# Graph attention on one core: a second chain of accumulating DMAs, later steps for what waits on transfers, and small matrix products in place of transposes

## The chip, the cores and the metric

One core of a Trainium2 chip. The metric is the device time of one launch in microseconds (us). A core has five engines with a queue each: TensorE (PE in the profile, its weight loads PEld), VectorE (DVE), ScalarE (ACT), GpSimd (POOL) and SyncE (SP). Transfers run on 16 DMA engines, whichever queue issued them. The rounds ran on several chips, each with the kernel before beside the others; its median moved between 2603.27 and 2607.61 us, so a difference between two rounds is good to some 4 us.

## The reference

Two graph attention layers over 2048 nodes and 8 graphs, then a normalisation. The matrix of scores is 2048 x 2048 for each of the 8 graphs and 4 heads, and once more per graph in the second layer.

```python
def _gat_layer(h, mask, b):
    scores = einsum('...nd,...md->...nm', h, h)
    scores = where(mask, scores, NEG)
    attn = softmax(scores, axis=-1)
    return einsum('...nm,...md->...nd', attn, h) + b

mask = graph + eye(N) > 0
h    = einsum('bnc,hdc->bhnd', x, Wh)
cat  = heads side by side of _gat_layer(h, ...)
h2   = einsum('bnk,dk->bnd', leaky_relu(cat, 0.2), Wo)
z2   = leaky_relu(_gat_layer(h2, ...), 0.2)
out  = layernorm(z2) * gamma + beta
return layernorm(x + out)
```

## The kernel before

Two heads (or two graphs) are worked on together, each with 64 of the 128 partitions. A *step* `(c, m)` makes the scores of 128 nodes `m` against a *chunk* of 512 nodes `c`, subtracts the mask, takes the exponential `e` (128 x 1024, 512 KB), and, three steps later (`LAG`), multiplies it with the values into two PSUM banks `O[c]`. 16 steps are a chunk, four chunks a unit, and there are 16 units of the first layer and 4 of the second.

```python
def scores(self, c, m):
    ps = spsum(...)                                   # two PSUM buffers, tag "s"
    ... 4 matmuls of 64x64 on 64x512 into ps          # PE
    nc.vector.tensor_tensor(e, ps, mask[c]..., OP.subtract)      # DVE
    nc.scalar.activation(e, e, AF.Exp, ...)                      # ACT
    return e

def values(self, c, m, e):
    if m == 0:
        self.O[c] = [opsum(...) for r in range(2)]    # banks last used by chunk c - 2
    ... 4 matmuls into self.O[c][r]
```

The softmax needs the sum of `e` over all `m`. It is brought down to a few terms first, in two ways at once: GpSimd adds tiles (2.4 us each), and an accumulating DMA adds one tile onto another in SBUF (0.9 us of GpSimd to issue). A DMA onto a chain's first tile must wait for the one before it on the same tile.

```python
CHAINS = (((0, 3, 6, 9, 12),), ((0, 4, 8, 12), (2, 6, 10, 14)))     # first, second layer
...
def add_up(self, c, m, e):
    for k, chain in enumerate(CHAINS[self.second]):
        if m == chain[0]:
            self.first[k] = e; self.terms[c].append(e); return
        if m in chain:
            nc.gpsimd.dma_start(out=self.first[k], in_=e, accum_op=OP.add); return
    ... else nc.gpsimd.tensor_tensor(self.acc, self.acc, e, OP.add)
```

The rest of a chunk is done by jobs that are placed so many steps after its start, among the steps of the next chunks. `sums` multiplies the terms with ones; four small DMAs of 2 KB (`zt`) spread the result over partitions; `invert` takes the reciprocal, which goes to DRAM (`rd`) and comes back broadcast (`z`, 128 KB); `scale` multiplies `O[c]` by it. `project`, then `keep` (first layer) or `norm` (second layer) finish, and they are the last to read `O[c]`.

```python
LATE = [(19, "join"), (20, "join2"), (21, "fifth"), (21, "sums"), (22, "leaky"), (25, "invert"),
        (29, "scale"), (31, "project"), (32, "keep")]
NORM = [32, 33, 34, 36, 42, 43, 45, 46, 47, 50]
for t in range(total + 64):
    ... scores of step t;  values and add_up of step t - LAG;  then the jobs placed at t
```

Of the kernel before, what the change touches and what calls it, by code (L numbers as in the profile page):

```python
# [354 lines left out]
def fast_kernel(ctx: ExitStack, tc: tile.TileContext, x, adj, Wh, bh, Wo, bo, gamma, beta, out, flag):  # L355
# [14 lines left out]
    CHAINS = (((0, 3, 6, 9, 12),), ((0, 4, 8, 12), (2, 6, 10, 14)))  # L370
# [18 lines left out]
    def opsum(name):  # L389
        return psum.tile([P, W], F32, tag="o", name=name, bufs=4)  # L390
# [40 lines left out]
    def load_x(bp):  # L431
        sts = []
        for h in range(2):
            st = slot([P, NB // 2, 2, C], F32, f"x{bp}_{h}")
            for b2 in range(2):
                nc.sync.dma_start(out=st[:, :, b2, :],
                                  in_=x[2 * bp + b2, h * N // 2:(h + 1) * N // 2].rearrange("(c p) d -> p c d", p=P))
            sts.append(st)
        return sts

    def transpose_x(bp, sts, h):
        if h == 0:
            xT[bp] = big.tile([P, N], F32, tag="xT", name=f"xT{bp}", bufs=1)
        p = spsum(f"px{bp}_{h}")
        for k in range(NB // 2):
            nc.tensor.transpose(p[:, k * P:(k + 1) * P], sts[h][:, k].rearrange("p b d -> p (b d)"), ident)
        nc.scalar.copy(xT[bp][:, h * 1024:(h + 1) * 1024], p)

    x0 = load_x(0)
# [40 lines left out]
    for q in range(HP):  # L490
        nc.tensor.transpose(pw[:, q * P:(q + 1) * P], wst[:, q].rearrange("p r c -> p (r c)"), ident)
        nc.tensor.transpose(pw[:, 256 + q * D:256 + (q + 1) * D], wos[:, q * P:(q + 1) * P], ident[:D, :D])
    nc.vector.tensor_copy(whT, pw[:, :H * D])
    nc.vector.tensor_copy(woT.rearrange("p q d -> p (q d)"), pw[:, 256:256 + HP * D])
# [17 lines left out]
    class Unit:  # L512
# [6 lines left out]

        def prepare(self, h):  # L520

            n = self.n
            if h == 0:
                self.hT = h2T[self.bp] if self.second else maps[self.bp, self.hp][:, self.b2, :]
                self.hN = big.tile([P, NB, P], F32, tag="hN", name=f"hN{n}")
            p = spsum(f"pn{n}_{h}")
            for k in range(NB // 2):
                m = h * NB // 2 + k
                nc.tensor.transpose(p[:, k * P:(k + 1) * P], self.hT[:, m * P:(m + 1) * P], ident)  # L529
            b = bob.rearrange("p r d -> p (r d)") if self.second else bhb[:, self.hp * P:(self.hp + 1) * P]  # L530
            nc.vector.tensor_add(self.hN[:, h * NB // 2:(h + 1) * NB // 2, :], p.rearrange("p (m d) -> p m d", d=P),  # L531
                                 b.unsqueeze(1).to_broadcast([P, NB // 2, P]))
# [13 lines left out]
        def values(self, c, m, e):  # L546
            if m == 0:
                self.O[c] = [opsum(f"o{self.n}_{c}_{r}") for r in range(2)]
            for j in range(2):
                for r in range(2):  # L550
                    rows = slice(r * 64, (r + 1) * 64)
                    nc.tensor.matmul(self.O[c][r][j * D:(j + 1) * D, :], self.hN[rows, m, j * D:(j + 1) * D],  # L552
                                     e[rows, j, :], start=(m == 0), stop=(m == NB - 1))

        def add_up(self, c, m, e):

            if m == 0:
                self.terms[c], self.first, self.acc = [], {}, None
            for k, chain in enumerate(CHAINS[self.second]):
                if m == chain[0]:  # L560
                    self.first[k] = e
                    self.terms[c].append(e)
# [8 lines left out]
            elif len(self.terms[c]) == len(CHAINS[self.second]):  # L571
                acc = accs.tile([P, 2, W], F32, tag="acc", name=f"acc{self.n}_{c}")
                nc.gpsimd.tensor_tensor(acc, self.acc, e, OP.add)  # L573
                self.acc = acc
                self.terms[c].append(acc)
            else:
                nc.gpsimd.tensor_tensor(self.acc, self.acc, e, OP.add)  # L577


        def join(self, c):  # L580

            a, b = self.O[c]
            t = wtile(f"oj{self.n}_{c}")
            nc.scalar.copy(t, a)  # L584
            self.t = t

        def join2(self, c):
            b = self.O[c][1]
            nc.vector.tensor_tensor(b, b, self.t, OP.add)  # L589

        def fifth(self, c):
            self.t = wtile(f"o5{self.n}_{c}")
            nc.scalar.mul(self.t, self.O[c][1], SLOPE)  # L593

        def leaky(self, c):
            b = self.O[c][1]
# [253 lines left out]
```

## Time and profile before

| | before |
|---|---|
| time | 2607.61 us (4 runs, 2600.8 to 2609.52) |
| PE busy / POOL busy | 96% / 85% |
| accumulating DMAs, landing after | 352, 4.9 us |
| the reciprocal's way: zt / rd / z, landing after | 1.8 / 1.4 / 3.6 us |
| first score / last value product / end | 25.7 / 2555.8 / 2604.0 us |

PE sets the pace: between the first score and the last value product it does two groups of eight matmuls per step, each 0.858 us, and any wait of PE is added to the time. Other engines matter where they make PE wait. The times from issue to landing in the DMA part of the page are medians.

### The profile page before, as it was taken

The numbers are of one execution on the slowest core, as the hardware profiler recorded it, in microseconds if no ns is written. First come the engines' busy times: TensorE is split into PE (matmuls) and PEld (weight loads), VectorE is DVE, ScalarE is ACT, GpSimd is POOL, SyncE is SP. The second block draws the span as 40 slices with busy tenths as digits, with TensorE's granted clock in tenths as the row PEclk, the third lists the DMA queues.
The fourth block names the chain that finished last, engine by engine and source line by source line (L and its number), as shares of the span: only waits on it lengthen the run. The fifth ranks groups of instructions, "written<-read, shape, count | busy, mean of one in ns | idle before, by whom it ended". The sixth has DMA issues, their size and how long they took to land.

```text
span 2604.0 us, 53831 instructions
## 1 busy us (share of the span) xinstructions
PE 2507.1 (96%) x22406; PEld 866.4 (33%) x22406; DVE 1834.2 (70%) x1813; ACT 1703.5 (65%) x1721; POOL 2214.6 (85%) x1249
## 2 busy tenths in 40 slices
PE   8999999999999999999999999999999999999993
PEld 3333333333333333333333333333333333333331
DVE  6877777677776677667767667766777777777773
ACT  6766666666666666666666666666666666666662
POOL 4779898788789998889868999888889898877996
PEclk9999999999999999999999999999999999999996
DMA  7644434334554443434455344433444443346663
GB/s 180 158 104 86 81 76 90 74 74 82 98 115 94 84 81 78 96 71 84 81 110 111 79 85 83 90 74 74 82 78 79 83 84 76 74 90 119 123 123 79
DMA packets 168991, 239.91 MB, mean 92 GB/s; under 512 B 96898, under 2 KB 113346, under 8 KB 168738
## 3 DMA queue, kind: packets, MB, share of 16 engines
q0 software_dynamic: 50864, 184.83, 37.8%
q1 hardware_dynamic: 117250, 51.36, 7.7%
q8 instruction: 177, 2.90, 0.5%
q14 instruction: 76, 0.62, 0.1%
q10 hardware_dynamic: 624, 0.20, 0.0%
HBM read 46.60 MB, written 4.52 MB: 20 GB/s over the span
## 4 chain that ended last, share of the span: by engine, by line
PE 67%; DMA 9%; POOL 5%; DVE 5%; issue 3%; ACT 3%; SPq 1%; DVEq 0%; ACTq 0%; POOLq 0%
PE s L539 32%; PE o L552 29%; DVE e L542 4%; DMA z<-rd 4%; PE pz L609 3%; POOL acc L577 3%; DMA rd<-rt 2%; DMA e<-e 2%; DMA zt<-zsb 1%; PE pn L529 1%; ACT e L543 1%; PE o L653 1%; POOL st L691 1%; SPq L618 1%; POOL y L692 1%
## 5 line engine op out<-in xcount | busy, mean ns | idle before, releaser
L543 ACT ACTIVATE e<-e,shifts 128x1024 f32<-128x1024 f32 x1280 | 1469.3, 1149 | 823.5 <-DVE e L542 801.4
L542 DVE TENSOR_TENSOR e<-s,mask 128x1024 f32<-128x1024 f32 x1280 | 1558.8, 1221 | 588.6 <-PE s L539 566.6
L577 POOL TENSOR_TENSOR acc<-acc,e 128x1024 f32<-128x1024 f32 x656 | 1605.5, 2447 | 129.8 <-ACT e L543 104.7
L552 PE MATMUL o<-e,hN 64*64 64x512 f32 x10240 | 1332.3, 591 | 0.0
L539 PE MATMUL s<-hT 64*64 64x512 f32 x8192 | 1078.5, 597 | 24.9 <-DVE e L542 22.1
L552 PEld LDWEIGHTS o<-e,hN 64*64 64x64 f32 x10240 | 392.0, 133 | 710.5 <-issue 515.4
L539 PEld LDWEIGHTS s<-hT 64*64 64x64 f32 x8192 | 289.9, 133 | 611.5 <-issue 378.5
L565 POOL DMA_DIRECT2D e<-e x352 | 320.7, 911 | 48.6 <-ACT e L543 25.4
L573 POOL TENSOR_TENSOR acc<-e,e 128x1024 f32<-128x1024 f32 x80 | 189.8, 2372 | 106.1 <-ACT e L543 99.2
L539 PE MATMUL s<-h2T 64*64 64x512 f32 x2048 | 268.8, 595 | 3.9 <-DVE e L542 3.9
L539 PEld LDWEIGHTS s<-h2T 64*64 64x64 f32 x2048 | 74.3, 133 | 147.1 <-issue 115.1
L609 PE MATMUL pz<-e,ones 128*32 128x512 f32 x448 | 100.1, 610 | 10.1 <-DMA e<-e 7.2
L636 DVE TENSOR_TENSOR z<-o,z 128x512 f32<-128x512 f32 x80 | 54.9, 687 | 72.1 <-DMA z<-rd 72.0
L609 PE MATMUL pz<-acc,ones 128*32 128x512 f32 x320 | 85.0, 610 | 9.4 <-POOL acc L577 9.4
L691 POOL TENSOR_TENSOR st<-st,mhalf 128x8 f32<-128x8 f32 x32 | 56.9, 1777 | 41.6 <-ACT st L690 41.4
L589 DVE TENSOR_TENSOR o<-o,oj 128x512 f32<-128x512 f32 x80 | 55.9, 699 | 4.5 <-ACT oj L584 2.8
L612 ACT COPY zsb<-pz 128x512 f32<-128x512 f32 x80 | 46.2, 578 | 19.0 <-PE pz L609 19.0
L597 DVE TENSOR_TENSOR o<-o,o 128x512 f32<-128x512 f32 x80 | 55.2, 690 | 0.7 <-ACT o L593 0.7
L487 DVE CAST mask<-pm 128x1024 uint8<-128x1024 bf16 x32 | 39.1, 1223 | 16.4 <-PE pm L486 15.3
L593 ACT ACTIVATE o<-o 128x512 f32<-128x512 f32 x80 | 46.3, 578 | 0.8 <-DVE o L589 0.8
L584 ACT COPY oj<-o 128x512 f32<-128x512 f32 x80 | 45.5, 569 | 0.3
L531 DVE TENSOR_TENSOR hN<-pn,bhb 128x1024 f32<-128x1024 f32 x32 | 39.1, 1223 | 8.6 <-PE pn L529 7.8
(72 smaller groups left out, 616.6 us busy)
## 6 DMA issues: line engine op xcount, KB each, us to landing
e<-e POOLq DMA_DIRECT2D x352, 512.0 KB, 4.9
z<-rd SPq DMA_DIRECT2D x160, 128.0 KB, 3.6
adj<-in_adj_dram SPq DMA_DIRECT2D x32, 512.0 KB, 7.8
zt<-zsb SPq DMA_DIRECT2D x320, 2.0 KB, 1.8
x<-in_x_dram SPq DMA_DIRECT2D x16, 256.0 KB, 6.6
xr<-in_x_dram SPq DMA_DIRECT2D x32, 128.0 KB, 5.6
out_dram<-y SPq DMA_DIRECT2D x32, 128.0 KB, 2.1
rd<-rt SPq DMA_DIRECT2D x80, 4.0 KB, 1.4
```

Of the source, the lines that this page charges most:

```text
L539: nc.tensor.matmul(ps[k * 64:(k + 1) * 64, j, :], self.hT[rows, m * P + k * 64:m * P + (k + 1) * 64], self.hT[rows, c * W:(c + 1) * W], st ...
L542: nc.vector.tensor_tensor(e, ps, mask[c][:, m, :].unsqueeze(1).to_broadcast([P, 2, W]), OP.subtract)
L543: nc.scalar.activation(e, e, AF.Exp, bias=shifts[:, 1:2] if self.second else shifts[:, 0:1], scale=1.0)
L552: nc.tensor.matmul(self.O[c][r][j * D:(j + 1) * D, :], self.hN[rows, m, j * D:(j + 1) * D], e[rows, j, :], start=(m == 0), stop=(m == NB - 1))
L565: nc.gpsimd.dma_start(out=self.first[k], in_=e, accum_op=OP.add)
L573: nc.gpsimd.tensor_tensor(acc, self.acc, e, OP.add)
L577: nc.gpsimd.tensor_tensor(self.acc, self.acc, e, OP.add)
L589: nc.vector.tensor_tensor(b, b, self.t, OP.add)
L597: nc.vector.tensor_tensor(b, b, self.t, OP.max)
L609: nc.tensor.matmul(pz[q:q + 32, :W], ones, terms[s * half + k][:, j, :], start=(k == 0), stop=(k == half - 1), tile_position=(0, q))
L636: nc.vector.tensor_tensor(dst, self.O[c][1], self.z[c], OP.mult)
L691: nc.gpsimd.tensor_tensor(st[:, 2, :], st[:, 1, :], mhalf, OP.pow)
```

## The change

It means to relieve GpSimd by more accumulating DMAs (576 instead of 352), to give the transfers more steps to land, to avoid changes of TensorE's tiling by doing transposes and the centring as 64x64 products, and to start the steps earlier by placing the first map projections among them. Cut to its core:

```diff
-    CHAINS = (((0, 3, 6, 9, 12),), ((0, 4, 8, 12), (2, 6, 10, 14)))
+    CHAINS = (((0, 3, 6, 9, 12), (1, 5, 8, 11)), ((0, 3, 6, 9, 12), (1, 4, 7, 10, 13)))
+    JOINED = (1, 2)                      # first layer: GpSimd adds the second chain to its own sum
...
-        return psum.tile([P, W], F32, tag="o", name=name, bufs=4)
+        return psum.tile([P, 2, W], F32, tag="o", name=name)
...
+    def turn(dst, src, rows):
+        nc.tensor.matmul(dst, src, ident[rows, rows], start=True, stop=True)
...  prepare: 8 transposes of 128x128 become 32 products of 64x64; centring and x likewise
-        nc.scalar.copy(xT[bp][:, h * 1024:(h + 1) * 1024], p)
+        nc.scalar.copy(xT[bp][:, h * 1024:(h + 1) * 1024].rearrange("c (r p k) -> c r k p", r=2, p=64), pv)
...
+            any_ = nc.vector if self.n == len(units) - 1 and c == NC - 1 else nc.gpsimd   # last norm on DVE
...
+    at(0, lambda: project_x(0, 0, 1))    # first projections and transposes among the steps
...
-    LATE = [(19, "join"), (20, "join2"), (21, "fifth"), (21, "sums"), (22, "leaky"), (25, "invert"), (29, "scale"), (31, "project"),
-            (32, "keep")]
-    NORM = [32, 33, 34, 36, 42, 43, 45, 46, 47, 50]
+    LATE = [(19, "join"), (20, "join2"), (21, "fifth"), (22, "leaky"), (22, "sums"), (26, "invert"), (31, "scale"),
+            (33, "project"), (34, "keep")]
+    NORM = [34, 35, 36, 37, 46, 47, 53, 54, 55, 62]
...  the check of the sums (judge) moves ahead of the last norm
```

More of the change, by code (lines that the diff above doesn't have):

```diff
@@ L429, in fast_kernel, with load_x, transpose_x @@
     xT = {}
-    def load_x(bp):
-        sts = []
-        for h in range(2):
-            st = slot([P, NB // 2, 2, C], F32, f"x{bp}_{h}")
-            for b2 in range(2):
-                nc.sync.dma_start(out=st[:, :, b2, :],
-                                  in_=x[2 * bp + b2, h * N // 2:(h + 1) * N // 2].rearrange("(c p) d -> p c d", p=P))
-            sts.append(st)
-        return sts
-    def transpose_x(bp, sts, h):
+    def turn(dst, src, rows):
+        nc.tensor.matmul(dst, src, ident[rows, rows], start=True, stop=True)
+    def load_x(bp, h):
+        st = slot([P, 2, NB // 2, C], F32, f"x{bp}_{h}")
+        for b2 in range(2):
+            nc.sync.dma_start(out=st[:, b2], in_=x[2 * bp + b2, h * N // 2:(h + 1) * N // 2].rearrange("(p k) d -> p k d", p=P))
+        return st
+    def transpose_x(bp, st, h):
         if h == 0:
@@ L444, in transpose_x @@
         p = spsum(f"px{bp}_{h}")
+        pv = p.rearrange("c (r k p) -> c r k p", r=2, p=64)
         for k in range(NB // 2):
-            nc.tensor.transpose(p[:, k * P:(k + 1) * P], sts[h][:, k].rearrange("p b d -> p (b d)"), ident)
-        nc.scalar.copy(xT[bp][:, h * 1024:(h + 1) * 1024], p)
-    x0 = load_x(0)
+            for b2 in range(2):
+                for r in range(2):
+                    rows = slice(r * 64, (r + 1) * 64)
+                    turn(pv[b2 * C:(b2 + 1) * C, r, k, :], st[rows, b2, k, :], rows)
+        nc.scalar.copy(xT[bp][:, h * 1024:(h + 1) * 1024].rearrange("c (r p k) -> c r k p", r=2, p=64), pv)
+    x0 = [load_x(0, h) for h in range(2)]
     ws = slot([P, 1024], F32, "ws")
@@ L490, in fast_kernel @@
     for q in range(HP):
-        nc.tensor.transpose(pw[:, q * P:(q + 1) * P], wst[:, q].rearrange("p r c -> p (r c)"), ident)
-        nc.tensor.transpose(pw[:, 256 + q * D:256 + (q + 1) * D], wos[:, q * P:(q + 1) * P], ident[:D, :D])
-    nc.vector.tensor_copy(whT, pw[:, :H * D])
-    nc.vector.tensor_copy(woT.rearrange("p q d -> p (q d)"), pw[:, 256:256 + HP * D])
+        nc.tensor.transpose(pw[:, 0, q * P:(q + 1) * P], wst[:, q].rearrange("p r c -> p (r c)"), ident)
+        nc.tensor.transpose(pw[:, 1, q * D:(q + 1) * D], wos[:, q * P:(q + 1) * P], ident[:D, :D])
+    nc.vector.tensor_copy(whT, pw[:, 0, :H * D])
+    nc.vector.tensor_copy(woT.rearrange("p q d -> p (q d)"), pw[:, 1, :HP * D])
     maps = {}
@@ L518, in __init__, with hT @@
             self.terms, self.zt, self.z, self.O, self.ln = {}, {}, {}, {}, {}
+        @property
+        def hT(self):
+            return h2T[self.bp] if self.second else maps[self.bp, self.hp][:, self.b2, :]
         def prepare(self, h):
@@ L523, in prepare @@
             if h == 0:
-                self.hT = h2T[self.bp] if self.second else maps[self.bp, self.hp][:, self.b2, :]
                 self.hN = big.tile([P, NB, P], F32, tag="hN", name=f"hN{n}")
             p = spsum(f"pn{n}_{h}")
+            pv = p.rearrange("p (j m d) -> p j m d", j=2, d=D)
             for k in range(NB // 2):
                 m = h * NB // 2 + k
-                nc.tensor.transpose(p[:, k * P:(k + 1) * P], self.hT[:, m * P:(m + 1) * P], ident)
-            b = bob.rearrange("p r d -> p (r d)") if self.second else bhb[:, self.hp * P:(self.hp + 1) * P]
-            nc.vector.tensor_add(self.hN[:, h * NB // 2:(h + 1) * NB // 2, :], p.rearrange("p (m d) -> p m d", d=P),
-                                 b.unsqueeze(1).to_broadcast([P, NB // 2, P]))
+                for g in range(2):
+                    for j in range(2):
+                        rows = slice(j * D, (j + 1) * D)
+                        turn(pv[g * 64:(g + 1) * 64, j, k, :], self.hT[rows, m * P + g * 64:m * P + (g + 1) * 64], rows)
+            b = bob if self.second else bhb[:, self.hp * P:(self.hp + 1) * P].rearrange("p (j d) -> p j d", d=D)
+            nc.vector.tensor_add(self.hN[:, h * NB // 2:(h + 1) * NB // 2, :].rearrange("p m (j d) -> p j m d", d=D), pv,
+                                 b.unsqueeze(2).to_broadcast([P, 2, NB // 2, D]))
         def scores(self, c, m):
@@ L547, in values @@
             if m == 0:
-                self.O[c] = [opsum(f"o{self.n}_{c}_{r}") for r in range(2)]
+                self.O[c] = opsum(f"o{self.n}_{c}")
             for j in range(2):
@@ L551, in values @@
                     rows = slice(r * 64, (r + 1) * 64)
-                    nc.tensor.matmul(self.O[c][r][j * D:(j + 1) * D, :], self.hN[rows, m, j * D:(j + 1) * D],
+                    nc.tensor.matmul(self.O[c][j * D:(j + 1) * D, r, :], self.hN[rows, m, j * D:(j + 1) * D],
                                      e[rows, j, :], start=(m == 0), stop=(m == NB - 1))
@@ L557, in add_up @@
             if m == 0:
-                self.terms[c], self.first, self.acc = [], {}, None
+                self.first, self.acc, self.made = {}, None, False
+                self.terms[c] = []
             for k, chain in enumerate(CHAINS[self.second]):
@@ L561, in add_up @@
                     self.first[k] = e
-                    self.terms[c].append(e)
                     return
@@ L570, in add_up @@
                 self.acc = e
-            elif len(self.terms[c]) == len(CHAINS[self.second]):
+            elif not self.made:
                 acc = accs.tile([P, 2, W], F32, tag="acc", name=f"acc{self.n}_{c}")
                 nc.gpsimd.tensor_tensor(acc, self.acc, e, OP.add)
-                self.acc = acc
-                self.terms[c].append(acc)
+                self.acc, self.made = acc, True
             else:
                 nc.gpsimd.tensor_tensor(self.acc, self.acc, e, OP.add)
+            if m == NB - 1:
+                k = JOINED[self.second]
+                for chain in range(k, len(self.first)):
+                    nc.gpsimd.tensor_tensor(self.acc, self.acc, self.first[chain], OP.add)
+                self.terms[c] += [self.first[j] for j in range(k)] + [self.acc]
         def join(self, c):
-            a, b = self.O[c]
-            t = wtile(f"oj{self.n}_{c}")
-            nc.scalar.copy(t, a)
-            self.t = t
+            self.t = wtile(f"oj{self.n}_{c}")
+            nc.scalar.copy(self.t, self.O[c][:, 0, :])
         def join2(self, c):
-            b = self.O[c][1]
+            b = self.O[c][:, 1, :]
             nc.vector.tensor_tensor(b, b, self.t, OP.add)
@@ L592, in fifth @@
             self.t = wtile(f"o5{self.n}_{c}")
-            nc.scalar.mul(self.t, self.O[c][1], SLOPE)
+            nc.scalar.mul(self.t, self.O[c][:, 1, :], SLOPE)
         def leaky(self, c):
-            b = self.O[c][1]
+            b = self.O[c][:, 1, :]
             nc.vector.tensor_tensor(b, b, self.t, OP.max)
@@ L635, in scale @@
             dst = self.z[c] if self.second or self.hp else z0[:, self.b2, c, :]
-            nc.vector.tensor_tensor(dst, self.O[c][1], self.z[c], OP.mult)
+            nc.vector.tensor_tensor(dst, self.O[c][:, 1, :], self.z[c], OP.mult)
         def project(self, c):
-            p = self.O[c][0]
             if self.second:
                 for i in range(CB):
-                    nc.tensor.matmul(p[:, i * P:(i + 1) * P], self.z[c][:, i * P:(i + 1) * P],
-                                     centre.rearrange("p r d -> p (r d)"), start=True, stop=True)
+                    for g in range(2):
+                        for b2 in range(2):
+                            rows = slice(b2 * D, (b2 + 1) * D)
+                            nc.tensor.matmul(self.O[c][g * 64:(g + 1) * 64, b2, i * D:(i + 1) * D],
+                                             self.z[c][rows, i * P + g * 64:i * P + (g + 1) * 64], centre[rows, b2, :],
+                                             start=True, stop=True)
                 return
+            p = self.O[c][:, 0, :]
             if self.hp == 0 or c % 2 == 0:
@@ L662, in keep @@
                 k = c - 1 + g
-                nc.scalar.copy(h2T[self.bp][rows, k * W:(k + 1) * W], self.O[c][0][g * D:(g + 1) * D, :])
+                nc.scalar.copy(h2T[self.bp][rows, k * W:(k + 1) * W], self.O[c][g * D:(g + 1) * D, 0, :])
         def norm(self, c, part):
@@ L674, in norm @@
                 self.y = ytile(f"y{n}_{c}")
-                nc.scalar.copy(self.y, self.O[c][0])
+                o = self.O[c][:, :, :W // 2]
+                nc.scalar.copy(self.y.rearrange("p (b i) -> p b i", b=2), o)
                 self.sq = wtile(f"sq{n}_{c}")
-                nc.scalar.square(self.sq, self.O[c][0])
+                nc.scalar.square(self.sq.rearrange("p (b i) -> p b i", b=2), o)
                 self.st = small.tile([P, 6, K], F32, tag="st", name=f"st{n}_{c}", bufs=2)
                 self.xr = ytile(f"xr{n}_{c}")
-                xv = self.xr.rearrange("p (i b d) -> p i b d", b=2, d=D)
+                xv = self.xr.rearrange("p (b i d) -> p b i d", b=2, d=D)
                 for b2 in range(2):
-                    nc.sync.dma_start(out=xv[:, :, b2, :],
+                    nc.sync.dma_start(out=xv[:, b2],
                                       in_=x[2 * self.bp + b2, c * W:(c + 1) * W, :].rearrange("(i p) d -> p i d", p=P))
@@ L691, in norm @@
                 nc.gpsimd.tensor_tensor(st[:, 2, :], st[:, 1, :], mhalf, OP.pow)
-                nc.gpsimd.tensor_tensor(v(y), v(y), col(st[:, 2, :]), OP.mult)
+                any_.tensor_tensor(v(y), v(y), col(st[:, 2, :]), OP.mult)
             elif part == 3:
-                nc.gpsimd.tensor_tensor(v(y), v(y), row(gam), OP.mult)
-                nc.gpsimd.tensor_tensor(v(y), v(y), row(bet), OP.add)
-                nc.gpsimd.tensor_tensor(y, y, xr, OP.add)
+                any_.tensor_tensor(v(y), v(y), row(gam), OP.mult)
+                any_.tensor_tensor(v(y), v(y), row(bet), OP.add)
+                any_.tensor_tensor(y, y, xr, OP.add)
             elif part == 4:
@@ L700, in norm @@
                 nc.scalar.mul(st[:, 4, :], st[:, 3, :], -1.0 / D)
-                nc.gpsimd.tensor_tensor(v(y), v(y), col(st[:, 4, :]), OP.add)
+                any_.tensor_tensor(v(y), v(y), col(st[:, 4, :]), OP.add)
             elif part == 6:
@@ L705, in norm @@
             elif part == 9:
-                yv = y.rearrange("p (i b d) -> p i b d", b=2, d=D)
+                yv = y.rearrange("p (b i d) -> p b i d", b=2, d=D)
                 for b2 in range(2):
                     nc.sync.dma_start(out=out[2 * self.bp + b2, c * W:(c + 1) * W, :].rearrange("(i p) d -> p i d", p=P),
-                                      in_=yv[:, :, b2, :])
+                                      in_=yv[:, b2])
     order = []
@@ L740, in mask_job, with judge @@
             mask_turn(*pieces[k - AHEAD - 1], rowed.pop(k - AHEAD - 1))
-    done = 0
-    for _ in range(AHEAD):
-        mask_job(done)
-        done += 1
-    for h in range(2):
-        transpose_x(0, x0, h)
-    for q in range(NC):
-        project_x(0, 0, q)
-    for _ in range(3):
-        mask_job(done)
-        done += 1
-    for h in range(2):
-        units[0].prepare(h)
-    for i, k in enumerate(range(done, len(pieces) + AHEAD + 1)):
+    FIRST = AHEAD + 2
+    transpose_x(0, x0[0], 0)
+    for k in range(FIRST):
+        mask_job(k)
+        if k == AHEAD:
+            project_x(0, 0, 0)
+    at(0, lambda: project_x(0, 0, 1))
+    at(1, lambda: units[0].prepare(0))
+    at(2, lambda: transpose_x(0, x0[1], 1))
+    at(4, lambda: project_x(0, 0, 2))
+    at(5, lambda: project_x(0, 0, 3))
+    at(7, lambda: units[0].prepare(1))
+    for i, k in enumerate(range(FIRST, len(pieces) + AHEAD + 1)):
         at(2 * i, lambda k=k: mask_job(k))
     xst = {}
-    LATE = [(19, "join"), (20, "join2"), (21, "fifth"), (21, "sums"), (22, "leaky"), (25, "invert"), (29, "scale"), (31, "project"),
-            (32, "keep")]
-    NORM = [32, 33, 34, 36, 42, 43, 45, 46, 47, 50]
+    LATE = [(19, "join"), (20, "join2"), (21, "fifth"), (22, "leaky"), (22, "sums"), (26, "invert"), (31, "scale"),
+            (33, "project"), (34, "keep")]
+    NORM = [34, 35, 36, 37, 46, 47, 53, 54, 55, 62]
+    def judge():
+        tot = small.tile([P, 4], F32, tag="tot", name="tot", bufs=1)
+        nc.vector.tensor_reduce(tot[:, 0:1], zall.rearrange("p c k -> p (c k)"), AX.X, OP.add)
+        nc.vector.tensor_reduce(tot[:, 1:2], zall.rearrange("p c k -> p (c k)"), AX.X, OP.min)
+        nc.vector.tensor_scalar(tot[:, 0:1], tot[:, 0:1], math.exp(LOG_TOP), None, OP.is_lt)
+        nc.vector.tensor_scalar(tot[:, 1:2], tot[:, 1:2], math.exp(LOG_LOW), None, OP.is_gt)
+        nc.vector.tensor_mul(tot[:, 2:3], tot[:, 0:1], tot[:, 1:2])
+        pf = opsum("pf")
+        nc.tensor.matmul(pf[0:1, 0, 0:1], tot[:, 2:3], ones[:, 0:1], start=True, stop=True)
+        fl = small.tile([1, 1], I32, tag="fl", name="fl", bufs=1)
+        nc.vector.tensor_scalar(fl, pf[0:1, 0, 0:1], P - 0.5, None, OP.is_lt)
+        nc.sync.dma_start(out=flag, in_=fl)
+    at(total - NB + 27, judge)
     es = {}
-    for t in range(total + 64):
+    for t in range(total + 80):
         if t < total:
@@ L779, in fast_kernel @@
                         if c == 0:
-                            xst[v.bp] = load_x(v.bp)
+                            xst[v.bp] = [load_x(v.bp, h) for h in range(2)]
                         elif c == 1:
                             for h in range(2):
-                                at(t + 2 + 4 * h, lambda v=v, h=h: transpose_x(v.bp, xst[v.bp], h))
+                                at(t + 2 + 4 * h, lambda v=v, h=h: transpose_x(v.bp, xst[v.bp][h], h))
                     if lead and c == 2:
@@ L797, in fast_kernel @@
     assert not jobs
-    tot = small.tile([P, 4], F32, tag="tot", name="tot", bufs=1)
-    nc.vector.tensor_reduce(tot[:, 0:1], zall.rearrange("p c k -> p (c k)"), AX.X, OP.add)
-    nc.vector.tensor_reduce(tot[:, 1:2], zall.rearrange("p c k -> p (c k)"), AX.X, OP.min)
-    nc.vector.tensor_scalar(tot[:, 0:1], tot[:, 0:1], math.exp(LOG_TOP), None, OP.is_lt)
-    nc.vector.tensor_scalar(tot[:, 1:2], tot[:, 1:2], math.exp(LOG_LOW), None, OP.is_gt)
-    nc.vector.tensor_mul(tot[:, 2:3], tot[:, 0:1], tot[:, 1:2])
-    pf = opsum("pf")
-    nc.tensor.matmul(pf[0:1, 0:1], tot[:, 2:3], ones[:, 0:1], start=True, stop=True)
-    fl = small.tile([1, 1], I32, tag="fl", name="fl", bufs=1)
-    nc.vector.tensor_scalar(fl, pf[0:1, 0:1], P - 0.5, None, OP.is_lt)
-    nc.sync.dma_start(out=flag, in_=fl)
 def gat_kernel(tc: tile.TileContext, x, adj, Wh, bh, Wo, bo, gamma, beta, out):
```

## The prediction

> **What bounds the kernel now.** I read the page first, then the matmul engine's timeline over whole chunks, then the waits, then the chain of waits near the end. A step is one 128-row block of scores, its mask, exponential and value products; 16 steps make a chunk, 4 chunks a unit, 20 units (16 of the first layer, 4 of the second) give 1280 steps.
>
> ```profile
> PE 2507.1 (96%) x22406; PEld 866.4 (33%) x22406; DVE 1834.2 (70%) x1813; ACT 1703.5 (65%) x1721; POOL 2214.6 (85%) x1249
> ...
> L577 POOL TENSOR_TENSOR acc<-acc,e 128x1024 f32<-128x1024 f32 x656 | 1605.5, 2447 | 129.8 <-ACT e L543 104.7 <-PE pz L609 0.9
> ...
> L565 POOL DMA_DIRECT2D e<-e x352 | 320.7, 911 | 48.6 <-ACT e L543 25.4 <-issue 10.9 <-DMA e<-e 10.8
> ```
>
> TensorE (PE) is busy throughout; GpSimd (POOL), at 85%, is next. The timeline gives the price of each job to PE, as the distance between two starts:
>
> ```profile
> 614.88 1.04 PE L552 MATMUL o<-e,hN 64*64 64x512 f32 x8
> 615.84 0.62 PE L609 MATMUL pz<-e,ones 128*32 128x512 f32 x2
> ...
> 616.84 1.09 PE L539 MATMUL s<-hT 64*64 64x512 f32 x8
> 617.75 1.04 PE L552 MATMUL o<-e,hN 64*64 64x512 f32 x8
> ...
> 636.81 1.04 PE L552 MATMUL o<-e,hN 64*64 64x512 f32 x8
> 637.78 1.09 PE L529 MATMUL pn<-ident,h2T 128*128 128x128 f32 x8
> 638.80 1.09 PE L539 MATMUL s<-hT 64*64 64x512 f32 x8
> 639.71 1.04 PE L552 MATMUL o<-e,hN 64*64 64x512 f32 x8
> ```
>
> Undisturbed groups of eight start 0.858 us apart, so the steps alone cost 1280 x 2 x 0.858 = 2197 us. A sum chain in the first layer costs 616.84 - 614.88 - 0.86 = 1.10 us (64 of them), in the second 1.96 (738.41 - 735.59 - 0.86; 16): 101 us. Half a transposition of the map costs 638.80 - 636.81 - 0.86 = 1.13, and 0.05 more for the late start after it: 38 among the steps, 45 us. Projections between the layers: 574.85 - 572.01 - 0.86 = 1.98, 16 times: 32. Map projections 24, mask turns 27, centring 726.10 - 724.04 - 0.86 = 1.20, 15 times: 18; input transposes 7. Together 254 us. The first score starts at 25.7 and the last value product ends at 2555.8, so the head is 25.7 and the tail 48.2 us. 2197 + 254 + 74 = 2525; the remaining 79 us are waits and small restarts.
>
> ```profile
> DVE z L636 <- DMA z<-rd: 72.0, 40, 4.5
> ...
> PE s L539 <- DVE e L542: 26.0, 25, 4.9
> ...
> POOL e L565 <- DMA e<-e: 10.8, 10, 2.7
> ...
> PE pz L609 <- POOL acc L577: 9.4, 4, 3.6
> ```
>
> VectorE (DVE) stands 72 us for the reciprocals that come back from DRAM. Only what exceeds the double buffer of score banks (about 1.2 us, less the 0.7 us product itself) reaches PE: going through the starts, the lengthened distances after a late z add up to some 30 us, and those where PE waits for Pool's sum, an accumulating DMA or a late norm (801 to 863, 1439 to 1515 and 2440 us) to some 27 us.
>
> **What the Trainium skill says.** "TensorEngine Tiling (Array Packing)", Key Properties: a change of tiling mode drains TensorE. The trace agrees: from 64x64 to 128x128 the transposes start 0.11 us late, and the values after the next scores 0.05 late. "DMA: Bandwidth & Descriptors", Anatomy of one DMA: about 2 us fixed plus bytes at 436 GB/s, 3.2 us for 512 KB; here an accumulating one takes 4.9 us, so the measured figure is used. The same page, Queues, rings and completion order: every DMA engine takes turns between the queues that have work; so more accumulation slows the reciprocals' transfers. The trace agrees: z takes 3.2 us between 200 and 560 us (accumulating queue 35.5% busy) and 4.1 between 2310 and 2550 (52.5%). "PSUM — Partial Sum Buffer", bank collisions: a bank that one engine reads must not be written by TensorE, so a matmul into a reused bank waits for the reader. That decides below.
>
> **The change, part by part.**
> Pool: a first-layer chunk had 10 additions and 4 issues, 10 x 2.43 + 4 x 0.91 = 28 us in some 30; now 6 + 1 additions and 7 issues, 23.4. Second layer: 6 and 6 (20 us) become 4 and 8 (17), beside 10 us of norm. The PE count of the sums stays (2 and 4 terms). In the first layer Pool stopped PE hardly at all, so little comes from it there; in the second, with the norm parts spread further (46, 47, 53 to 55, 62), most of the 27 us should go: -22.
> Later placements: scale moves from 29 to 31 steps, invert from 25 to 26, sums from 21 to 22. That leaves one step (1.7 us) more for the reciprocal to land. But 576 accumulating DMAs instead of 352 raise that queue from 37.8% to about 62% (estimate, in proportion), and z and rd should take 1 us longer together. I count -18 of 30.
> Products of 64x64: 32 per half map, 8 in turn on each of four tiles. A 512-column product takes 0.858, so a 64-column one 0.107: 0.86 us at best; if the two weight loads of each (133 ns recorded) do not hide, up to 1.7. I take 1.05 against 1.18: -5 over 38. Centring, 4 in turn per tile, about 0.65 against 1.25: -9. Inputs: -1.
> Head: scores may start near 16 instead of 26, but about 7 us of products then sit among the first 8 steps, with waits for maps: -3. Tail: the last accumulating DMA is one step earlier and Pool less behind, so the sums end some 6 us after the last value instead of 10.8 (2566.5 - 2555.8): -5; norm on DVE, five operations of 0.7 instead of 1.04 to 1.27: -2.4; centring at a cold clock -1; the flag written before the norm -3. Sum -11.
> Against it: keep and the first norm part move from 32 to 34. The output bank is taken by the chunk after next at step 35 (32 + lag 3), and now only one step lies between. The timeline of before shows the slack:
>
> ```profile
> 725.01 1.16 PE L643 MATMUL o<-centre,z 128*128 128x128 f32 x8
> ...
> 726.10 1.09 PE L539 MATMUL s<-h2T 64*64 64x512 f32 x8
> ...
> 729.64 0.56 ACT L675 COPY y<-o 128x512 f32<-128x512 f32 x1
> ...
> 730.11 0.60 ACT L677 ACTIVATE sq<-o 128x512 f32<-128x512 f32 x1
> ...
> 732.16 1.04 PE L552 MATMUL o<-e,hN 64*64 64x512 f32 x8
> ```
>
> The copies end at 730.7 and the new value group starts at 732.16: 1.45 us of slack. They stand behind the exponential of their own step on ScalarE (ACT), which ends some 3.6 us after that step's scores start; two steps (3.43 us) later the slack is -2.0. For keep (ends 580.03, next value group 580.91) it is 0.88, so -2.5. 14 norms and 16 keeps: 68 us of new PE waiting. They sit just ahead of the next chunk's sums and give Pool and DMA time, so I count 60.
> Sum: -22 - 18 - 15 - 14 + 60 = -9. I add 3 for accumulations that queue on each other in the second layer: 2600. The rest of the reasoning below moves it down to 2594.
>
> **The rivals.** (1) The bank wait does not appear, or is short: then the sum is about -69, 2537 us. For it: the placements look as if tried on a chip. Against it: the order of ACT's work and the bank's next use are fixed by the code. I give it a small weight, which takes 6 us off. (2) DMA becomes a bound: in the second layer two accumulations now come in every three steps, 5.15 us, while 37.8% of 2604 over 352 is 2.8 us of engines each, 5.6 for two. Pool, in order, then waits on the previous link, sums come late and z too. For it: that arithmetic. Against it: at 52.5% the landing rose only from 4.8 to 5.2. It would add 20 to 40 us: 2630. (3) The small products cost their weight loads: 1.7 instead of 1.18 in 40 halves, +20. Against it: loads of 64 columns are hidden among the steps now.
>
> **Range and chances.** Gains of about 69 and losses of about 60 are each uncertain by some 25 us; together 35 on either side, so 2545 to 2635 about 2594. 2% is 52 us: below 2554 with 0.18, above 2659 with 0.06, between with 0.76.
>
> **What would show it.** Right: in the waits, PE o waiting for ACT (y, sq or h2T copies) some 30 times by about 2 us; DVE z waiting for its DMA well under 72; gaps of PE at 801 to 863 gone; Pool near 75%; the accumulating queue near 60%; the half maps 0.9 to 1.2 us with no late start; tail near 37. Wrong: no such bank wait and a span under 2550; or Pool waiting for e<-e by over 100 us; or half maps over 1.5 us.

## The result

The changed kernel takes 2748.41 us (4 runs, 2736.48 to 2752.37) against 2607.61: a ratio of 1.0537 with a 95% interval of 1.0497 to 1.0577, 5.4% slower. A ratio is the mean time of one kernel's fast runs over that of the other's fast runs of the same rounds, so it is not quite the ratio of the medians.

The page of the changed kernel, engines and DMA part:

```profile
PE 2526.9 (92%) x25478; PEld 875.3 (32%) x25478; DVE 1845.3 (67%) x1819; ACT 1708.0 (62%) x1721; POOL 1874.5 (69%) x1243
...
q0 software_dynamic: 83120, 302.29, 59.3%
...
e<-e POOLq DMA_DIRECT2D x576, 512.0 KB, 5.6
z<-rd SPq DMA_DIRECT2D x160, 128.0 KB, 4.8
...
zt<-zsb SPq DMA_DIRECT2D x320, 2.0 KB, 4.3
...
rd<-rt SPq DMA_DIRECT2D x80, 4.0 KB, 2.9
```

GpSimd was relieved, from 85% to 69%, and the time grew: in the kernel before PE had waited only 9.4 us, four times, for a sum that GpSimd made. The accumulating queue holds the DMA engines for 59.3% of the span, and all three transfers of the reciprocal land later: z by 1.2 us, zt by 2.5, rd by 1.5 (how much of this is the chains' shows in e1 below). The waits of the changed kernel (who waited for whom, us in total, times, longest):

```profile
POOL e L578 <- DMA e<-e: 205.8, 117, 4.4
...
DVE z L651 <- DMA z<-rd: 127.0, 65, 5.5
...
PE s L552 <- DVE e L555: 47.0, 44, 5.6
DVE zall L640 <- DMA zt<-zsb: 46.7, 39, 11.9
...
DVE e L555 <- DMA e<-e: 32.5, 16, 4.1
...
PE o L565 <- ACT h2T L682: 30.8, 16, 2.3
...
PE o L565 <- ACT sq L697: 25.4, 14, 2.0
```

The first row is new in size: GpSimd, which works in order, stands 206 us in front of the next link of a chain, where before it was 10.8. DVE waits for z 127 us instead of 72. And the last two rows did not exist: PE waits for a PSUM bank that ACT still reads, 16 times for `keep` and 14 times for the norm's copies, 56 us.

The timeline of the changed kernel around one `keep` shows that wait (engine, line, number in the group, and in brackets the idle time before):

```profile
602.92 1.15 ACT L556 ACTIVATE e<-e,shifts 128x1024 f32<-128x1024 f32 x1 [1.86 <-DVE e L555]
...
604.08 1.17 ACT L682 COPY h2T<-o 64x512 f32<-64x512 f32 x2
...
605.30 1.09 PE L565 MATMUL o<-e,hN 64*64 64x512 f32 x8 [2.06 <-ACT h2T L682]
```

The copies stand behind the exponential of their own step, end at 605.25, and only then may the chunk after next write the bank.

Where did the 131 us of the two profiled spans (2734.7 - 2604.0) come from? I went through the starts of PE's groups and took 0.858 us off each distance; what is left is charged to what stood between, or to a wait. From the first score to the last value product:

| us | before | after |
|---|---|---|
| start to the first score | 25.7 | 17.0 |
| late value products (bank waits and restarts) | 21 | 88 |
| late scores | 36 | 70 |
| sums, with their waits | 120 | 135 |
| half maps and x, mask turns, projections, centring, map projections | 157 | 185 |
| last value product to the end | 48.2 | 44.7 |

The new bank wait (+67) and the late scores (+34) are most of it. The jobs that left the head come back as 28 us among the steps, for 9 us less before them, though part of that growth is again waiting.

Some of these times are not idle time but slow work. The trace records the granted clock at one half in 20 spells of 3.4 to 10.2 us ahead of the last 60 us of the changed kernel, 85.3 us in all, and in 5 spells, 27.3 us, before. Each of the 20 begins during a wait of PE or within 3 us after one. Here is one of them (clock 0.50 between 1110.2 and 1113.4 us): groups start 1.71 us apart instead of 0.858.

```profile
1109.09 1.09 PE L552 MATMUL s<-hT 64*64 64x512 f32 x8 [3.87 <-DVE e L555]
1110.00 1.81 PE L565 MATMUL o<-e,hN 64*64 64x512 f32 x8
1111.57 1.95 PE L552 MATMUL s<-hT 64*64 64x512 f32 x8
1113.28 1.17 PE L565 MATMUL o<-e,hN 64*64 64x512 f32 x8
```

Half of the difference, some 29 us of the 131, is an estimate of what the waits cost on top of their own length. The spells, with those of the last 60 us, also make up the lower mean clock of the changed kernel, 0.976 against 0.987.

### The profile page after: what moved, and what is told of

It reads as the page before. It is cut to its first block, busy times and chain, and to the rows that moved or that the text cites. A ratio compares the mean times of both kernels' runs of the same rounds, so it can differ in the third digit from the quotient of the medians.

```text
span 2734.7 us, 60106 instructions
## 1 busy us (share of the span) xinstructions
PE 2526.9 (92%) x25478; PEld 875.3 (32%) x25478; DVE 1845.3 (67%) x1819; ACT 1708.0 (62%) x1721; POOL 1874.5 (69%) x1243
## 3 DMA queue, kind: packets, MB, share of 16 engines
q0 software_dynamic: 83120, 302.29, 59.3%
## 5 line engine op out<-in xcount | busy, mean ns | idle before, releaser
L565 PE MATMUL o<-e,hN 64*64 64x512 f32 x10240 | 1346.6, 596 | 56.2 <-ACT h2T L682 30.8
L589 POOL TENSOR_TENSOR acc<-acc,e 128x1024 f32<-128x1024 f32 x368 | 917.6, 2493 | 137.2 <-ACT e L556 121.0
L578 POOL DMA_DIRECT2D e<-e x576 | 511.4, 899 | 545.7 <-ACT e L556 209.2
L552 PEld LDWEIGHTS s<-hT 64*64 64x64 f32 x8192 | 296.6, 134 | 627.5 <-issue 406.5
L586 POOL TENSOR_TENSOR acc<-e,e 128x1024 f32<-128x1024 f32 x80 | 195.7, 2446 | 57.9 <-ACT e L556 55.1
L593 POOL TENSOR_TENSOR acc<-acc,e 128x1024 f32<-128x1024 f32 x64 | 151.4, 2366 | 5.0
L651 DVE TENSOR_TENSOR z<-o,z 128x512 f32<-128x512 f32 x80 | 55.2, 690 | 127.3 <-DMA z<-rd 127.0
L713 POOL TENSOR_TENSOR st<-st,mhalf 128x8 f32<-128x8 f32 x32 | 59.3, 1853 | 57.6 <-ACT st L712 57.6
```

The costliest lines, as they stand in the source:

```text
L552: nc.tensor.matmul(ps[k * 64:(k + 1) * 64, j, :], self.hT[rows, m * P + k * 64:m * P + (k + 1) * 64], self.hT[rows, c * W:(c + 1) * W], st ...
L565: nc.tensor.matmul(self.O[c][j * D:(j + 1) * D, r, :], self.hN[rows, m, j * D:(j + 1) * D], e[rows, j, :], start=(m == 0), stop=(m == NB - 1))
L586: nc.gpsimd.tensor_tensor(acc, self.acc, e, OP.add)
L593: nc.gpsimd.tensor_tensor(self.acc, self.acc, self.first[chain], OP.add)
L713: nc.gpsimd.tensor_tensor(st[:, 2, :], st[:, 1, :], mhalf, OP.pow)
```

## The experiments

All ran on the chip; each ratio is against the kernel before in the same rounds.

**1 to 4: which part?** The changed kernel with old chains, with the old step table, with both, and the kernel before with new chains only.

```diff
# e1_old_chains, on the changed kernel; e3_both_old has this and the next
-    CHAINS = (((0, 3, 6, 9, 12), (1, 5, 8, 11)), ((0, 3, 6, 9, 12), (1, 4, 7, 10, 13)))
+    CHAINS = (((0, 3, 6, 9, 12),), ((0, 4, 8, 12), (2, 6, 10, 14)))
# e2_old_steps, on the changed kernel
-    LATE = [... (22, "sums"), (26, "invert"), (31, "scale"), (33, "project"), (34, "keep")];  NORM = [34, 35, ...]
+    LATE = [... (21, "sums"), (25, "invert"), (29, "scale"), (31, "project"), (32, "keep")];  NORM = [32, 33, ...]
# e4_chains_alone, on the kernel before: the new CHAINS, JOINED and add_up
```

> The changed kernel with the chains of before (352 accumulating DMAs instead of 576), all else as changed. Theory: the loss of 141 us is the bank wait (56 us of PE idle behind the ACT copies, measured) and the crowding by the second chain (the rest). Then this run keeps the bank wait, near 56 us, loses the DMA part, z waits fall below 60 us and the time is 2660 to 2690. Rival A, the placements and products do it all, the chains nothing: 2730 to 2750. Rival B, the chains do it all: near 2607.

> The changed kernel with the old step table (scale 29, project 31, keep and first norm part 32, and so on), second chain kept. Theory: the bank wait goes to nearly 0 (-56 us), but the reciprocals, slowed by the accumulations (4.8 us instead of 3.6), are now asked for one step earlier after their start, so DVE's wait for z grows from 127 to over 200 us and eats most of it: 2700 to 2750. Rival A (placements do it all): 2610 to 2640.

> The changed kernel with old chains and the old step table: the 64x64 products, the jobs moved from the head among the steps, the tail. Theory: these are worth little either way, 2595 to 2625, with no bank wait and z waits near 72 us. Rival C, the products and the moved jobs cost much: 2640 to 2680.

> The kernel before with nothing but the new chains. Theory: the crowding shows by itself: accumulating queue near 60% busy, z landing near 4.8 us, DVE waiting for z over 200 us, time 2680 to 2730. Rival A: within 1% of 2607.

| run | chains | steps | us | ratio, 95% interval |
|---|---|---|---|---|
| changed | new | new | 2748.41 | 1.0537 (1.0497 to 1.0577) |
| e1_old_chains | old | new | 2642.65 | 1.0144 (1.0123 to 1.0165) |
| e2_old_steps | new | old | 2780.24 | 1.0672 (1.0650 to 1.0694) |
| e3_both_old | old | old | 2614.26 | 1.0037 (1.0015 to 1.0059) |
| e4_chains_alone (rest as before) | new | old | 2781.72 | 1.0677 (1.0642 to 1.0713) |

The chains cost 106 us with the new steps (2748.41 - 2642.65) and 166 to 176 with the old ones (2780.24 - 2614.26; 2781.72 - 2605.82, its own before). Both single-cause rivals fall: with old chains the kernel is neither near 2748 nor near 2607. My figures for e1, e2 and e4 were too mild: e1 is 17 us faster than its range, e2 and e4 are 30 and 52 us slower than theirs. The later steps cost 28 us with the old chains and gain 32 with the new: they help against late transfers and hurt by the bank. Everything else in the change (e3) is nearly neutral with the old steps, +0.4%. The transfers of e1_old_chains, with no second chain:

```profile
z<-rd SPq DMA_DIRECT2D x160, 128.0 KB, 4.4
...
zt<-zsb SPq DMA_DIRECT2D x320, 2.0 KB, 2.6
...
rd<-rt SPq DMA_DIRECT2D x80, 4.0 KB, 1.4
```

So most of z's delay in the changed kernel came with the other parts of the change. The chains add 0.4 us to z, 1.7 to zt and 1.5 to rd with the new steps; with the old ones (e4 against the kernel before: z 3.8, zt 4.5, rd 3.0) 0.2, 2.7 and 1.6. The waits of e4_chains_alone:

```profile
DVE z L641 <- DMA z<-rd: 227.1, 79, 8.7
...
PE s L540 <- DVE e L543: 121.7, 74, 7.6
DVE zall L630 <- DMA zt<-zsb: 116.0, 61, 11.0
```

DVE now waits for z in 79 of 80 chunks, and 116 us for zt, and this reaches PE as 122 us in front of scores (26 in the kernel before).

**5 and 6: the bank wait by itself.** `keep` and the first norm part one step earlier, at 33, directly behind `project`. They are then ahead of the next exponential in ACT's order, and no engine does anything else.

```diff
# e5_keep_33_old_chains on e1_old_chains, e6_keep_33_new_chains on the changed kernel
-            (33, "project"), (34, "keep")]
-    NORM = [34, 35, 36, 37, 46, 47, 53, 54, 55, 62]
+            (33, "project"), (33, "keep")]
+    NORM = [33, 35, 36, 37, 46, 47, 53, 54, 55, 62]
```

> The first of the four runs with old chains and new steps (2642.65 us), with keep and the first norm part one step earlier, at 33, right behind the projection and so ahead of the next exponential in ACT's order. Theory: the bank wait (57 us of PE idle in that run) goes to under 5 us and the time to 2585 to 2600, below the kernel before. Rival: the copies then hold up the exponentials, or other waits take the place: 2620 or more.

> The changed kernel with only keep and the first norm part at 33. Theory: 56 us of bank wait go, but PE was in part waiting for transfers at the same time, so 2695 to 2720. Rival: the bank wait was hiding the transfers, which come out in full: 2735 or more.

2576.78 us (ratio 0.9891, 0.9874 to 0.9907) and 2678.28 us (1.0284, 1.0267 to 1.0301). One step is worth 66 us with old chains and 70 with new. I had expected less in the second case, in the belief that part of the bank wait overlapped with others; it did not, and both runs were faster than the ranges given for them. The spells at half clock also shrink, from 34.1 to 17.1 us with old chains and from 85.3 to 58.0 with new (counted as above); half of that, 9 and 14 us, on top of 57 and 56 us of idle time, is an estimate that comes near the two gains (in e6 4.6 us of bank wait are left). In e5 no row of PE waiting for the `h2T` or `sq` copies is left, while in e1 it was:

```profile
PE o L565 <- ACT h2T L682: 30.9, 16, 2.3
PE o L565 <- ACT sq L697: 26.5, 14, 2.1
...
DVE z L651 <- DMA z<-rd: 11.6, 8, 2.4
```

The same rows show the good side of the later steps: with old chains DVE waits only 11.6 us for z, against 72 before. e5 is the first kernel here that beats the one before.

**7: bytes, or issues and order?** e4_chains_alone, with half the columns in each accumulating DMA. 576 issues, their links and GpSimd's additions stay. The sums and the result are wrong; to keep the values finite the copy of the sums gives a constant.

```diff
-                    nc.gpsimd.dma_start(out=self.first[k], in_=e, accum_op=OP.add)
+                    nc.gpsimd.dma_start(out=self.first[k][:, :, :W // 2], in_=e[:, :, :W // 2], accum_op=OP.add)
-            nc.scalar.copy(zsb, pz[:, :W])
+            nc.scalar.activation(zsb, pz[:, :W], AF.Identity, bias=shifts[:, 4:5], scale=0.0)   # 1e35
```

> The kernel before with the new chains (2781.72 us), where each accumulating DMA moves half the columns; the sums and the result are wrong on purpose, and the sums are replaced by a constant to stay finite. 576 issues, their order and links and Pool's work stay. Theory, the bytes on the DMA engines delay the reciprocals' transfers: DVE's wait for z falls from 227 to under 110 us, zt lands in under 2.5 us, 2600 to 2650. Rival D, the number of issues and Pool's order do it: z waits stay over 180 us and the time over 2730.

2577.96 us (ratio 0.9888, 0.9872 to 0.9905), 204 us less than with whole bytes, and faster than I had said. The transfers of this run:

```profile
e<-e POOLq DMA_DIRECT2D x576, 256.0 KB, 4.2
z<-rd SPq DMA_DIRECT2D x160, 128.0 KB, 3.5
...
zt<-zsb SPq DMA_DIRECT2D x320, 2.0 KB, 2.8
...
rd<-rt SPq DMA_DIRECT2D x80, 4.0 KB, 1.4
```

Against e4, rd falls from 3.0 to 1.4 us, zt from 4.5 to 2.8 (under 2.5 was expected) and z, hardly delayed there, from 3.8 to 3.5; DVE's wait for z falls from 227.1 to 36.4 us. So the number of issues does not cost the time; the bytes in the DMA engines do. By which way is not shown by this run, since shorter transfers also shorten GpSimd's waits for a link, from 163.3 to 44.0 us. The 30 us by which it beats the kernel before are not the worth of the second chain either: all its accumulations together move 151 MB, against 185 MB before.

**8 and 9: head, products and tail.** e8 is e5 with the old head and the old loading and transposing of x. e9 is the kernel before with nothing but the step table of e5.

```diff
# e8_old_head on e5: load_x, transpose_x and the code ahead of the steps as before
# e9_steps_alone on the kernel before
-    LATE = [... (21, "sums"), (22, "leaky"), (25, "invert"), (29, "scale"), (31, "project"), (32, "keep")]
-    NORM = [32, 33, 34, 36, 42, 43, 45, 46, 47, 50]
+    LATE = [... (22, "leaky"), (22, "sums"), (26, "invert"), (31, "scale"), (33, "project"), (33, "keep")]
+    NORM = [33, 35, 36, 37, 46, 47, 53, 54, 55, 62]
```

> As the run with old chains and keep at 33, with the old head and the old input transposes (one 128x128 transpose and an ACT copy of 1.0 us instead of 2.0). Theory: the moved head saves 8.5 us at the start and gives back about 12 among the steps, so this is 0 to 8 us faster. Rival: the moved head is worth its 8 us: slower by 5 to 10.

> The kernel before with nothing but the new step table, keep and the first norm part at 33. It splits what the best run so far (old head, old chains, 2575.84 us) gains: if the placements are the whole gain, 2575 to 2583; if the 64x64 products and the tail carry their predicted 15 + 11 us, 2595 to 2605. My estimate: placements 20 us, 2583 to 2592.

2575.84 us (0.9877, 0.9860 to 0.9893) and 2587.95 us (0.9924, 0.9907 to 0.9940). The moved head is worth nothing: e8 and e5 differ by 0.9 us. The steps alone gain 18 us; the rest of the change without the moved head (small products of the maps and the centring, the norm on DVE, the earlier check, the output banks in pairs and the layouts that follow) gains another 12 (2587.95 - 2575.84). With the old steps that same rest, with the moved head, cost 0.4% (e3), so its worth depends on the steps; why was not looked into. e8_old_head is the fastest kernel. These two lines are ACT's copy of the transposed input, first of e5, then of e8:

```profile
L453 ACT COPY xT<-px 128x1024 f32<-128x1024 f32 x8 | 16.2, 2028 | 8.9 <-PE px L434 8.7
```

```profile
L452 ACT COPY xT<-px 128x1024 f32<-128x1024 f32 x8 | 8.1, 1012 | 9.6 <-PE px L451 9.5
```

The changed layout of x makes the copy write every eighth float, and it takes 2.0 us instead of 1.0, which is part of what the early start gives back: PE waits 5.9 us for this copy in e5, and not at all in e8.

**10: the chains in the second layer only.** e8 with the new chains in the 16 chunks of the second layer, where GpSimd has the norm to do as well.

```diff
-    CHAINS = (((0, 3, 6, 9, 12),), ((0, 4, 8, 12), (2, 6, 10, 14)))
+    CHAINS = (((0, 3, 6, 9, 12),), ((0, 3, 6, 9, 12), (1, 4, 7, 10, 13)))
```

> As the run with the old head, with the new chains in the second layer's 16 chunks only: 8 accumulating DMAs and 4 additions there instead of 6 and 6. Theory of a bound by accumulated bytes: two accumulations in three steps crowd there as in the first layer, so 5 to 20 us slower than 2575.84. Rival: in the second layer Pool is the bound beside the norm, and relief there pays: 5 to 15 us faster.

2601.08 us (0.9974, 0.9953 to 0.9995): 25 us slower than e8 by 32 more DMAs, more than I had put it at. Relieving GpSimd does not pay even there.

**11: more, but how many?** Meant as six accumulating DMAs in a first-layer chunk instead of four. By my mistake the 6th step belongs to the first chain already, so only one was added: 416 in all, not 480.

```diff
# on e5_keep_33_old_chains
-    CHAINS = (((0, 3, 6, 9, 12),), ...)
+    CHAINS = (((0, 3, 6, 9, 12), (1, 6, 11)), ...)
```

> As the run with old chains and keep at 33 (352 accumulating DMAs, 2576.78 us), with a second chain of three (1, 6, 11) in the first layer: 480 DMAs, between that and the 576 of the run of 2678.28. If the loss grows in proportion to the bytes: 2635 to 2640. Theory: it sets in once two accumulations overlap for long stretches, so here less than in proportion: 2590 to 2625, DVE's wait for z 30 to 70 us.

2586.42 us (0.9922, 0.9906 to 0.9939), 10 us over e5 for 64 more DMAs, where the remaining 160 up to e6 cost 92 us. Its expectation was for another number and is not tested by it. It left open whether the number counts or the distance between them.

**12 and 13: number or spacing?** Two kernels with 480 DMAs each, the same number of links and the same GpSimd additions; one issues an accumulation every second step, the other two in every three.

```diff
# on e5_keep_33_old_chains: e12_six_even, then e13_six_crowded
+    CHAINS = (((0, 3, 7, 11), (1, 5, 9, 13)), ...)
+    CHAINS = (((0, 3, 6, 9), (1, 4, 7, 10)), ...)
```

> As the run with old chains and keep at 33 (2576.78 us), with six accumulating DMAs in a first-layer chunk instead of four, at the 3rd, 5th, 7th, 9th, 11th and 13th step: one every 3.43 us. Theory of spacing: an accumulation (2.8 us of the engines, worked out from 38 percent of the span over 352) ends before the next begins, 2577 to 2600. Theory of number: with 480 DMAs about 2610 to 2640.

> As the run before this one, with the same six at the 3rd, 4th, 6th, 7th, 9th and 10th step: two in 5.15 us. Theory of spacing: Pool waits on the links, the reciprocals come late, at least 20 us slower than the even one, 2610 to 2650. Theory of number: the same as the even one within 10 us.

2578.61 us (0.9898, 0.9882 to 0.9915) and 2626.41 us (1.0083, 1.0067 to 1.0100). 128 more DMAs than e5 cost nothing when they are spread, and 50 us when they are crowded. The waits of e12, then those of e13:

```profile
DVE z L651 <- DMA z<-rd: 27.4, 16, 4.0
...
POOL e L578 <- DMA e<-e: 4.9, 5, 1.6
```

```profile
POOL e L578 <- DMA e<-e: 129.4, 83, 4.1
DVE z L651 <- DMA z<-rd: 85.2, 57, 4.8
```

With the same bytes in the whole span (accumulating queue at 52.2% and 51.6%) GpSimd waits 5 or 129 us for a link, zt lands after 2.9 or 4.2 us, and the spacing theory's ranges hold in both runs. It is the spacing that counts, not the number. 37.8% of 2604 us over 352 DMAs gives 2.8 us of all engines for one, an estimate from the profile of before: one every 3.43 us leaves room, two in 5.15 us do not. A rival inside this pair stays: the links of one chain are also four steps apart in e12 and three in e13. Three steps alone are not enough for a loss, for e5's single chain has them and its GpSimd waits 10.9 us for links; but a run with accumulations in adjacent steps and links four steps apart was not made. GpSimd's own additions are bunched at the end of the chunk in e13 as well; PE's waits for them, 12.7 us against 6.9, are too short for 48.

## Why the prediction was right or wrong

The prediction said 2594 us, within 2% at 0.76. The chip said 2748, outside the range. Step by step:

- **The bank wait: right.** It was put at 68 us from the slack in the old timeline, counted as 60; the profile shows 56 us of PE idle in 30 waits of up to 2.3 us, and undoing it gains 66 and 70 us, about the difference being work at half clock after the waits, which the prediction did not count. Counting it lower because it "gives Pool and DMA time" had no ground, as the step was worth as much with the crowded chains as without.
- **The crowding: this step failed.** The prediction took "-18 of 30" for the later placement and "+3" for accumulations that queue on each other, and gave rival (2) 20 to 40 us. The runs put it at 102 to 106 us with the new steps (e6 against e5, the changed kernel against e1). The sign of being wrong that it named itself, GpSimd waiting for links by over 100 us, came with 205.8. Two things were wrong in it. First, the arithmetic of two in 5.15 us against 5.6 was done for the second layer only. The first layer's chains (3, 5, 6, 8, 9, 11, 12) have the same rate, in 64 chunks instead of 16; e10 shows that the second layer's part is about 25 us. Second, it slowed only z and rd, by 1 us together. By the chains they lost 1.8 to 1.9 us, nearly all of it rd, and zt, a transfer of 2 KB that the prediction left out, 1.7 to 2.7. Together that is 3.6 to 4.5 us in medians on a path that was given one step, 1.7 us, more. The reading behind it, z at 3.2 us where the queue is 35.5% busy and at 4.1 where it is 52.5%, did not carry over: in the same two stretches zt lands after 1.8 us in both, and it was zt that the crowding slowed most.
- **"DMA becomes a bound" was judged by the wrong number.** Against it the prediction put that landing rose only from 4.8 to 5.2 us at 52.5% of the queue. A share over a window averages bursts and gaps; e12 and e13 have the same share and differ by 48 us.
- **The later steps, with transfers as they were: right in direction.** e9 gains 18 us; DVE's wait for z falls to 18.5 us there. -40 had been counted for this and for the waits on GpSimd together.
- **GpSimd's relief: wrong.** -22 was counted for the second layer; there the new chains cost 25. The waits that it meant to save did not go: PE waited 9.4 us in all for GpSimd's sums before and 20.0 after, four times each, and at 876.6 us still 5.83 us at once.
- **Small products: right for the maps.** Half a map takes 42.1 us over 40 in e3, 1.05 us, as predicted, with no late start after it. The centring was put at 0.65 and takes 0.91 (13.6 over 15). Rival (3), weight loads in the open, did not appear.
- **Head and tail: near zero.** The head was put at -3 and is 0. The tail was put at -11 and is -3.5 in the changed kernel: the predicted earlier end of the sums did not come, since PE waited 7.0 us for the last accumulating DMA.

What stays open: how much of the crowding's cost comes by the late reciprocals and how much by GpSimd's waits for links, which hold exponential tiles and showed as 32.5 us of DVE waiting for a tile. Both were large (links 129 us or more, z 85 or more) in every run with crowded chains of whole bytes in the first layer. One comparison separates them in part: from e2 to the changed kernel, by the later steps alone, DVE's waits for z and zt fall from 205.7 and 121.4 to 127.0 and 46.7 us, GpSimd's for links rise from 177.0 to 205.8, and the cost of the chains falls from 166 to 106 us. That puts some 60 us on the late reciprocals, by inference; the rest stays open.

## What to carry to other kernels

Moving work from a busy engine to DMA helps only if the DMA engines have room at the rate of the burst, not on the average: divide the engines' time for one transfer by the distance between two, and if it exceeds one (by the estimate of 2.8 us: 1.09 in e13, 0.82 in e12), spread them before adding more. Then look for the small, latency-bound transfers that share those engines, and count every hop of them. When a job is moved later, look for the next writer of what it reads: one step less of slack, or standing behind one more instruction in its engine's order, can cost a full wait each time, and here often a spell at half clock after it.

## What the Trainium skill lacked or had wrong

- "DMA: Bandwidth & Descriptors" has no figure for accumulating transfers from SBUF to SBUF, though it says that GpSimd's queue can issue them. Here 512 KB took 4.9 us to land and 256 KB 4.2 (the latter in a busier stretch), and one 512 KB transfer filled about 2.8 us of all engines (an estimate from the queue's share).
- The same page says that each DMA engine takes turns between queues, but not what it costs a tiny transfer: 2 KB landed in 1.8 to 2.6 us beside 352 accumulations and in 4.3 to 4.6 beside 576 crowded ones.
- No page gives the time of a strided ScalarE copy; writing every eighth float took 2.0 us instead of 1.0 for 128x1024.
